# A graph attention kernel: head 0's second weight sum on VectorE, a quarter of the destinations made in another place, clamp and rounding constant on ScalarE

## The chip, the cores and the metric

The kernel runs on one core of a Trainium2 chip. The metric is the device time of one launch in microseconds. Three runs of the kernel before took 617.31, 618.71 and 619.45 us; the median is 618.71. The profile comes from one further execution.

## The reference, cut to what matters

Two graph attention layers over 512 nodes and 16,896 edges (8,192 in both directions and a loop on each node), then a residual and a layer norm. The first layer has 8 heads of 768 features, the second has one.

```python
def gat_layer(x, W, a_s, a_d, b, edge_index, concat):
    h = (x @ W).reshape(n, H, C)
    src, dst = (edge_index[0], edge_index[1])
    alpha_s = jnp.einsum('nhc,hc->nh', h, a_s)
    alpha_d = jnp.einsum('nhc,hc->nh', h, a_d)
    e = jax.nn.leaky_relu(alpha_s[src] + alpha_d[dst], NEG_SLOPE)
    m = jax.ops.segment_max(e, dst, num_segments=n)
    e = jnp.exp(e - m[dst])
    denom = jax.ops.segment_sum(e, dst, num_segments=n)
    alpha = e / (denom[dst] + EPS)
    msg = h[src] * alpha[:, :, None]
    out = jax.ops.segment_sum(msg, dst, num_segments=n)
    ...
h = gat_layer(x, W1, a_src1, a_dst1, b1, edge_index, concat=True)
h = jax.nn.elu(h)
out = gat_layer(h, W2, a_src2, a_dst2, b2, edge_index, concat=True)
return _layernorm(x + out)
```

x is 512x768, W1 768x6144, W2 6144x768, all in float32.

## The kernel before, in words

**Dense form of the graph.** The kernel first counts the edges between every pair of nodes into a dense matrix `cnt` (4 tiles of 128 destinations, 512 sources) on TensorE, as products of one-hot matrices. From then on attention is dense: a score per pair, minus infinity where no edge is (`absent`), a softmax weighted by the counts, and a 512x512 matrix product per head.

**Heads.** For each head h three dense products follow one another: the projection x·W1 of the next head, the aggregation of this head (scores times features, then the ELU), and its part of the second layer's projection. All are done by Strassen-like schemes in halves (7 products P1 to P7 in place of 8) or thirds, so sums of blocks of both operands are made ahead of the matmuls: sums of x, of features and of scores on VectorE, sums of weight blocks on VectorE or by DMAs that add onto what stands in the tile (`accum_op=ALU.add`, issued from GpSimd's queue).

**The order around the change.** `tc.manual_schedule()` is on: each engine runs its instructions in the order in which the program writes them. Head 0's projection (`first_projection`, L644) and the edge counting are written out together, in the loop at L855 over five batches of edge chunks. For a batch, VectorE makes the destinations of a quarter of the chunks (`destinations`, L779: L776 and L781, into `od`) and the one-hot rows of sources (L796); ScalarE makes other one-hot rows for the next batch (L794); TensorE runs the products that are due (`wants`, L846: 3 of them by the end of batch 0, 8 by batch 1, and so on) and, after batches 2 and 4, the counting matmuls (L822). `ahead_of` (L843) holds what VectorE does before batch 1: `weight_sums` and the first sum of x (`s1`, L419), then come the fresh quarter of destinations, `s2` (L420) and `s4` (L422). Results of a product that VectorE has to add (L664) are kept in `waiting` and run at the start of the next batch; the one of batch 0 runs at its end.

**Head 0's weight sums.** The weights stand as `W1[0]`: the lower and the upper half of the rows (`lo`, `hi`), each with left and right columns (L, R). The sums are

- t1 (P5) = lo L + lo R, on VectorE (L580),
- t2 (P6) = t1 + hi R: hi R is loaded a second time into t2 (`sums_by_dma`, L262 to L266), and a DMA adds t1 (L268),
- P7 = lo R + hi R, by a DMA from the weights in HBM onto lo R (L582),
- t4 (P4) = t2 + hi L, by a DMA (L269).

After these, in GpSimd's queue, come head 1's sums (L113, L121, L268, L269 with `slot="w2"`). TensorE takes head 0's products in the order P1, P2, P5, P3, P6, P7, P4 (two groups of matmuls each, one per half of the nodes; the profile shows both as one row of twelve matmuls). P3 reads hi R and `s4`.

**Counts in digits.** The counting matmuls pack four digits to the base 64 in one float. `counted_in_digits` (L602) takes them apart: `higher` on ScalarE scales by a power of 64 and adds a large rounding constant (L614), takes the constant off again for the highest digit (L616); `lower` on VectorE takes it off the two middle digits (L621) and subtracts what belongs to the higher digit (L622); `mask` on ScalarE writes `absent`. One tile is done after batch 2, the other three after the last batch, interleaved with the first products of head 1 and the first scores of head 0 (L932 to L941).

**Between the count and the first aggregation.** The loop at L1222 runs head 1's products 4 to 13 and beside them head 0's softmax: `leak` (L719), `rank` (L724 and the exponential L730), `give` (L1214: the denominator on VectorE, scaling and parting into halves of words on ScalarE, L1015 and L1018, then a transposing DMA from SP, L1020), and `turn_in` (L1023, ScalarE puts the transposed scores together in `PT`). At n == 9 GpSimd clamps three quarters of `cnt` at zero from below (L1229). The first aggregation, `near_first` (L1115), starts with three products P1 (`begin`, each copied to `u` by ScalarE, L1132); after the first of them stands `turn_in(3)`; then the sums, P2 on top of each P1, and the rest. Its argument `fill` names work to be written at places (c, j) in it. The first reader of the clamped counts is `logarithm` (L736), in head 0's turn of the loop at L1292, for head 1.

Of the kernel before, what the change touches and what calls it, by code (L numbers as in the profile page):

```python
# [39 lines left out]
def gat_pass(  # L40
# [217 lines left out]
    def sums_by_dma(W_, m, slot):  # L258

        lo_, hi_, t1_ = W_  # L260
        t2, t4 = (w1_halves[j] if slot == "w1" else wpool.tile([P, HK, HALF], F32, name=f"{slot}t{j}") for j in (2, 4))
        loads = [(t2, R), (t4, L)]  # L262
        if slot == "w1":
            loads.insert(1, (hi_[:, :, R], R))
        for t_, cols in loads:
            nc.sync.dma_start(t_, block(m, 1, cols))  # L266

        additions = [lambda: nc.gpsimd.dma_start(t2, t1_, accum_op=ALU.add),  # L268
                     lambda: nc.gpsimd.dma_start(t4, t2, accum_op=ALU.add)]  # L269
        return dict(P1=lo_[:, :, L], P2=hi_[:, :, L], P3=hi_[:, :, R], P4=t4, P5=t1_, P6=t2,  # L270
                    P7=lo_[:, :, R]), additions

    B0, additions0 = sums_by_dma(W1[0], w1_0, "w1")
# [178 lines left out]
    def half(t, j, h=0):  # L452
        return lambda: half_logits(h, t)[j]()
# [123 lines left out]

    def weight_sums():

        nc.vector.tensor_tensor(W1[0][2], W1[0][0][:, :, L], W1[0][0][:, :, R], op=ALU.add)  # L580
        additions0[0]()
        nc.gpsimd.dma_start(W1[0][0][:, :, R], block(w1_0, 1, R), accum_op=ALU.add)  # L582
        additions0[1]()
        load_w1(1, "w2")()
        B_, additions1 = sums_by_dma(W1[1], w1[:, D:2 * D], "w2")
        for f in additions1:
            f()
        return B_
# [13 lines left out]
    def counted_in_digits(t, ps, steps):  # L602
# [9 lines left out]
        def higher():  # L612
            for j in range(NT - 1, 0, -1):
                nc.scalar.activation(c[:, j * P:(j + 1) * P], whole, AF.Copy, bias=ROUND, scale=scale / BASE ** j)  # L614
                if j == NT - 1:
                    nc.scalar.activation(c[:, j * P:], c[:, j * P:], AF.Copy, bias=-ROUND, accum_out=sums[:, NT + t:NT + t + 1])  # L616
            if not steps:
                nc.scalar.activation(c[:, :P], whole, AF.Copy, scale=scale)

        def lower():  # L620
            nc.vector.tensor_scalar(c[:, P:3 * P], c[:, P:3 * P], -ROUND, None, op0=ALU.add)  # L621
# [135 lines left out]
    if not general:  # L757
# [85 lines left out]
        ahead_of = {1: [lambda: B1.update(weight_sums()), s1]}  # L843
# [11 lines left out]
        for n, batch in enumerate(batches):  # L855
# [53 lines left out]
            if n == 0:  # L909
                waiting.pop()()  # L910
# [14 lines left out]
        def given_lift(t):  # L925
            q.append(lift(0, t))

        def order_of(*fs):
            for f, *args in fs:
                f(*args)  # L930

        second_tile, step_tile, last_tile = deferred  # L932
        order_of(second_tile[:1], (item, 16), (half(0, 1),), second_tile[1:2], step_tile[:1], (item, 17), (spread, 0),
                 (half(1, 1),), step_tile[1:2], (given_lift, 0), last_tile[:1], second_tile[2:], (half(2, 1),))
        leak(q[0])
        given_lift(1)
        rank(q[0], 0)
        order_of(last_tile[1:2], (half(3, 1),), step_tile[2:], (given_lift, 2))
        leak(q[1])
        rank(q[1], 1)  # L940
        order_of(last_tile[2:], (given_lift, 3))  # L941
    else:
# [12 lines left out]
        turn_b1()  # L955
        B1 = weight_sums()
# [265 lines left out]
    for n in range(4, 14):  # L1222
# [5 lines left out]
        if n == 9 and not general:  # L1228
            nc.gpsimd.tensor_scalar(cnt[:, :, :3 * P], cnt[:, :, :3 * P], 0.0, None, op0=ALU.max)  # L1229
# [62 lines left out]
    for h in range(H - 1):  # L1292
# [14 lines left out]
        if h == 0:  # L1307
            GA, gsums = left(gT, gS)
            finish = near_first(0, AA, BB, [*rsums, lsums[3]], {(0, 1): [half(2, 0, 1)], (1, 1): sources[:1], (2, 1): [*sources[1:], *row, targets[0]]},
# [356 lines left out]
```

## Time and profile before

| what | value |
|---|---|
| runs, median (lowest to highest) | 618.71 us (617.31 to 619.45) |
| profiled execution, its own time | 617.82 us |
| its span, first to last instruction | 615.9 us |
| granted TensorE clock | 0.999 |
| mean DMA rate over the span | 207 GB/s |

Engines have short names: PE is TensorE's matmuls and PEld its weight loads, DVE is VectorE, ACT is ScalarE, POOL is GpSimd, SP is SyncE. A name with a q is the engine's sequencer. Rows of a timeline show the start and the duration in microseconds, the engine, the line of the kernel, the operation, the tile written and those read (without buffer numbers), the shape, how many instructions were merged, and in brackets how long the engine stood idle before and what ended that. Rows of the chain show a start, a duration and what filled it. A waits row shows who waited for whom: microseconds in total, how many times, the longest. A group's row ends in busy time, the mean nanoseconds of one, and the idle time before.

### The profile page before, as it was taken

Reading aid. Unit: us, or ns where it says so; the run is one execution under the profiler, and the core shown is the slowest. Engines: PE = TensorE matmul, PEld = TensorE weight load, DVE = VectorE, ACT = ScalarE, POOL = GpSimd, SP = SyncE. Lnnn points to the kernel's source line nnn. Section 1 sums busy time; section 2 is a strip of 40 time slices with the busy share of each in tenths; the row PEclk is TensorE's granted clock in tenths of the full one; section 3 lists DMA queues with packets and bytes.
Section 4 is the critical chain, followed back from the end, with each engine's and each line's share of the span. In section 5 each row is a group of like instructions: output and inputs, shape, how many; then the busy total and the mean of one; then the engine's idle time right before and its main releaser. Section 6 shows DMA issues by size and latency. Waiting matters only on the chain.

```text
span 615.9 us, 8599 instructions
## 1 busy us (share of the span) xinstructions
PE 605.7 (98%) x2772; PEld 481.7 (78%) x2772; DVE 527.0 (86%) x1152; ACT 332.0 (54%) x623; POOL 150.4 (24%) x184
## 2 busy tenths in 40 slices
PE   9999999999999999999999999999999999999995
PEld 6565685557888888888888888888888888885553
DVE  6999989887999879977897879978898878978785
ACT  5557866812766164932757055741857056753360
POOL 3210301032431332403341332413342303110000
PEclk9999999999999999999999999999999999999999
DMA  8994968799999998999899999999889993690032
GB/s 296 315 245 79 228 160 277 150 304 312 230 176 233 252 247 221 143 314 245 182 182 219 256 257 220 135 315 210 207 204 213 288 287 69 153 270 6 17 78 80
DMA packets 107836, 127.42 MB, mean 207 GB/s; under 512 B 41558, under 2 KB 87946, under 8 KB 107018
## 3 DMA queue, kind: packets, MB, share of 16 engines
q1 hardware_dynamic: 75213, 90.83, 48.7%
q0 software_dynamic: 32208, 35.59, 37.6%
q8 instruction: 24, 0.39, 0.2%
q10 hardware_dynamic: 365, 0.40, 0.2%
q14 instruction: 26, 0.21, 0.1%
HBM read 97.81 MB, written 2.90 MB: 164 GB/s over the span
## 4 chain that ended last, share of the span: by engine, by line
PE 90%; DMA 4%; DVE 3%; ACT 2%; SPq 0%; issue 0%; DVEq 0%; POOLq 0%
PE mm L521 46%; PE mm L1086 18%; PE mm L439 14%; PE mm L1126 5%; PE mm L1611 3%; PE held L439 2%; DMA w1t<-w1t 2%; DMA w1t<-in_L_gnn_W_dram 1%; DMA zr<-pS 1%; DMA w1r<-in_L_gnn_W_dram 1%; DVE scr L448 1%; ACT PT L1023 1%; PE tr L822 0%; ACT pS L1018 0%; DVE q L719 0%
## 5 line engine op out<-in xcount | busy, mean ns | idle before, releaser
L527 ACT ACTIVATE hs<-mm 128x512 f32<-128x512 f32 x30 | 17.9, 596 | 81.2 <-PE mm L521 80.8
L1086 PE MATMUL mm<-PT,hs 128*128 128x256 f32 x216 | 52.5, 379 | 0.0
L728 ACT ACTIVATE q<-q,nmax 128x512 f32<-128x512 f32 x32 | 23.1, 721 | 49.1 <-DVE nmax L724 48.9
L534 DVE TENSOR_TENSOR hs<-hs,mm 128x512 f32<-128x512 f32 x45 | 30.9, 686 | 18.6 <-PE mm L521 17.8
L1086 PEld LDWEIGHTS mm<-PT,hs 128*128 128x128 f32 x216 | 41.0, 190 | 5.8
L532 POOL DMA_DIRECT2D h<-pass x22 | 26.7, 1312 | 76.3 <-ACT pass L531 75.6
L1023 ACT COPY PT<-zr 128x1024 uint16<-128x1024 uint16 x34 | 39.4, 1158 | 8.8 <-DMA zr<-pS 5.8
L534 DVE TENSOR_TENSOR h<-h,mm 128x512 f32<-128x512 f32 x56 | 38.3, 684 | 5.8 <-PE mm L521 5.6
L521 PE MATMUL mm<-w2r,xT 128*128 128x256 f32 x160 | 37.8, 379 | 0.0
L521 PE MATMUL mm<-w2r,gT 128*128 128x256 f32 x160 | 37.0, 379 | 0.0
L1086 PE MATMUL mm<-pS,gS 128*128 128x256 f32 x144 | 37.0, 379 | 0.0
L136 POOL DMA_DIRECT2D w1t<-in_L_gnn_W_dram x18 | 30.1, 1945 | 26.0 <-DVE pS L1059 26.0
L521 PE MATMUL mm<-w1t,hs 128*128 128x256 f32 x144 | 34.1, 380 | 0.0
L521 PE MATMUL mm<-w1r,hs 128*128 128x256 f32 x144 | 34.0, 379 | 0.0
L521 PE MATMUL mm<-w1r,gS 128*128 128x256 f32 x144 | 34.0, 379 | 0.0
L136 POOL DMA_DIRECT2D w1r<-in_L_gnn_W_dram x12 | 14.5, 1207 | 79.6 <-DMA w1r<-in_L_gnn_W_dram 75.9
L521 PEld LDWEIGHTS mm<-w2r,gT 128*128 128x128 f32 x160 | 30.4, 190 | 4.1
L521 PEld LDWEIGHTS mm<-w2r,xT 128*128 128x128 f32 x160 | 30.4, 190 | 4.1
L521 PEld LDWEIGHTS mm<-w1t,hs 128*128 128x128 f32 x144 | 27.3, 190 | 3.9 <-ACT absent L531 0.2
L1086 PEld LDWEIGHTS mm<-pS,gS 128*128 128x128 f32 x144 | 27.4, 190 | 3.7
L521 PEld LDWEIGHTS mm<-w1r,gS 128*128 128x128 f32 x144 | 27.3, 190 | 3.7
L521 PEld LDWEIGHTS mm<-w1r,hs 128*128 128x128 f32 x144 | 27.2, 190 | 3.8
(328 smaller groups left out, 1561.1 us busy)
## 6 DMA issues: line engine op xcount, KB each, us to landing
w2r<-in_L_gnn_W_dram SPq DMA_DIRECT2D x48, 384.0 KB
w1r<-in_L_gnn_W_dram SPq DMA_DIRECT2D x43, 384.0 KB
w1t<-in_L_gnn_W_dram SPq DMA_DIRECT2D x24, 256.0 KB
h<-pass POOLq DMA_DIRECT2D x22, 256.0 KB, 6.9
gT<-xd SPq DMA_DIRECT2D x5, 1024.0 KB
w1t<-in_L_gnn_W_dram POOLq DMA_DIRECT2D x18, 256.0 KB, 7.2
a_s<-in_L_gnn_a_src_dram SPq DMA_DIRECT2D x8, 384.0 KB
a_d<-in_L_gnn_a_dst_dram SPq DMA_DIRECT2D x8, 384.0 KB
```

The lines of the kernel that those rows point to most:

```text
L136: nc.gpsimd.dma_start(o, i, accum_op=ALU.add)
L439: nc.tensor.matmul(ps[:, :HALF], A_[p][:, k, i * P:(i + 1) * P], B_[p][:, k, :], start=start and k == 0, stop=k == HK - 1, skip_group_chec ...
L448: return [lambda al=al, a=a, sign=sign: nc.vector.scalar_tensor_tensor(scr, HS[h][:, t, :], sign, a, op0=ALU.mult, op1=ALU.mult, accum_out ...
L521: nc.tensor.matmul(bank[chain][:, i * TH:(i + 1) * TH], A_[p][:, k, i * P:(i + 1) * P], B_[p][:, k, :], start=first and i == k == 0, stop= ...
L527: nc.scalar.activation(out(o), ps, AF.Copy, scale=sign)
L532: nc.gpsimd.dma_start(out(o), part, accum_op=ALU.add)
L534: nc.vector.tensor_tensor(out(o), out(o), ps, op=ALU.add if sign > 0 else ALU.subtract)
L728: nc.scalar.activation(q, q, AF.Exp, bias=nmax, scale=-1.0, accum_out=dens[t])
L1023: nc.scalar.copy(PT.rearrange("p s n -> p (s n)").bitcast(U16).rearrange("p (s n h) -> p s n h", s=NT, h=2)[:, :, t * P:(t + 1) * P, :], p ...
L1086: nc.tensor.matmul(bank[p][:, :HN], A_[p][:, k, c * P:(c + 1) * P], B_[p][:, k, :], start=over is None and k == 0, stop=k == 1, skip_group ...
L1126: nc.tensor.matmul(banks[c, p][:, :HN], A_[p][:, k, c * P:(c + 1) * P], B_[p][:, k, :], start=over is None and k == 0, stop=k == 1, skip_g ...
L1611: nc.tensor.matmul(ps[:, :cols.stop - cols.start], PT[:, s, t * P:(t + 1) * P], h2[:, s, cols], start=(s == 2), stop=(s == 1))
```

## The change

Four edits:

1. For head 0, hi R is no longer loaded into t2. VectorE adds t1 and hi R into t2, in `weight_sums`. The first sum (t1) becomes a function of its own, `first_sum`; VectorE's order before batch 1 is now t1, `s1`, t2, and then `s2` and `s4`. GpSimd's queue loses the DMA that added t1.
2. The quarter of destinations that batch 1 needs is made at the end of batch 0, before the waiting addition of L664.
3. The rounding constant of the two middle digits is taken off by ScalarE (at the end of the loop in `higher`), not by VectorE.
4. The clamp of `cnt` is a Relu on ScalarE, written in `near_first` at place (0, 0), not a GpSimd instruction at n == 9. The calls after the last count stand in another order.

```diff
-    def sums_by_dma(W_, m, slot):
+    def sums_by_dma(W_, m, slot, by_vector=False):
...
         loads = [(t2, R), (t4, L)]
-        if slot == "w1":
+        if by_vector:
+            loads[0] = (hi_[:, :, R], R)
+        elif slot == "w1":
             loads.insert(1, (hi_[:, :, R], R))
...
-        additions = [lambda: nc.gpsimd.dma_start(t2, t1_, accum_op=ALU.add),
-                     lambda: nc.gpsimd.dma_start(t4, t2, accum_op=ALU.add)]
+        def sum_t2():
+            if by_vector:
+                nc.vector.tensor_tensor(t2, t1_, hi_[:, :, R], op=ALU.add)
+            else:
+                nc.gpsimd.dma_start(t2, t1_, accum_op=ALU.add)
+        additions = [sum_t2, lambda: nc.gpsimd.dma_start(t4, t2, accum_op=ALU.add)]
...
-    B0, additions0 = sums_by_dma(W1[0], w1_0, "w1")
+    B0, additions0 = sums_by_dma(W1[0], w1_0, "w1", by_vector=True)
...
+    def first_sum():
+        nc.vector.tensor_tensor(W1[0][2], W1[0][0][:, :, L], W1[0][0][:, :, R], op=ALU.add)
+
     def weight_sums():
 
-        nc.vector.tensor_tensor(W1[0][2], W1[0][0][:, :, L], W1[0][0][:, :, R], op=ALU.add)
         additions0[0]()
...
+            nc.scalar.activation(c[:, P:3 * P], c[:, P:3 * P], AF.Copy, bias=-ROUND)
             if not steps:
                 nc.scalar.activation(c[:, :P], whole, AF.Copy, scale=scale)
 
         def lower():
-            nc.vector.tensor_scalar(c[:, P:3 * P], c[:, P:3 * P], -ROUND, None, op0=ALU.add)
...
-        ahead_of = {1: [lambda: B1.update(weight_sums()), s1]}
+        ahead_of = {1: [first_sum, s1, lambda: B1.update(weight_sums())]}
...
             if n == 0:
+                ((k,),) = [sorted({c // quarter for c in batches[1]} - made)]
+                made.add(k)
+                destinations(k)
                 waiting.pop()()
...
-        order_of(second_tile[:1], (item, 16), (half(0, 1),), second_tile[1:2], step_tile[:1], (item, 17), (spread, 0),
-                 (half(1, 1),), step_tile[1:2], (given_lift, 0), last_tile[:1], second_tile[2:], (half(2, 1),))
-        leak(q[0])
-        given_lift(1)
-        rank(q[0], 0)
-        order_of(last_tile[1:2], (half(3, 1),), step_tile[2:], (given_lift, 2))
-        leak(q[1])
-        rank(q[1], 1)
-        order_of(last_tile[2:], (given_lift, 3))
+        order_of(second_tile[:1], (item, 16), (half(0, 1),), second_tile[1:2], step_tile[:1], (item, 17), (spread, 0), (half(1, 1),),
+                 (given_lift, 0), step_tile[1:2], last_tile[:1], second_tile[2:], (half(2, 1),), (given_lift, 1), (leak_at, 0),
+                 (rank_at, 0), last_tile[1:2], step_tile[2:], (half(3, 1),), (given_lift, 2), (leak_at, 1), (rank_at, 1),
+                 last_tile[2:], (given_lift, 3))
...
-        if n == 9 and not general:
-            nc.gpsimd.tensor_scalar(cnt[:, :, :3 * P], cnt[:, :, :3 * P], 0.0, None, op0=ALU.max)
...
+            def floor():
+                if not general:
+                    nc.scalar.activation(cnt[:, :, :3 * P], cnt[:, :, :3 * P], AF.Relu)
+
-            finish = near_first(0, AA, BB, [*rsums, lsums[3]], {(0, 1): [half(2, 0, 1)], (1, 1): sources[:1], (2, 1): [*sources[1:], *row, targets[0]]},
+            finish = near_first(0, AA, BB, [*rsums, lsums[3]], {(0, 0): [floor], (0, 1): [half(2, 0, 1)], (1, 1): sources[:1], (2, 1): [*sources[1:], *row, targets[0]]},
                                 [lambda: turn_in(3)])
```

`leak_at` and `rank_at` call `leak` and `rank` for a tile that exists by then.

More of the change, by code (lines that the diff above doesn't have):

```diff
@@ L926, in given_lift, with leak_at, rank_at @@
             q.append(lift(0, t))
+        def leak_at(t):
+            leak(q[t])
+        def rank_at(t):
+            rank(q[t], t)
         def order_of(*fs):
@@ L955, in gat_pass @@
         turn_b1()
+        first_sum()
         B1 = weight_sums()
```

## The prediction, made before the changed kernel was run

> **What bounds the kernel now.** I read the page first, then the waits of TensorE, then the chain that ended last, and only then the timelines of single engines around the two places that the waits name.
>
> ```profile
> span 615.9 us, 8599 instructions
> ...
> PE 605.7 (98%) x2772; PEld 481.7 (78%) x2772; DVE 527.0 (86%) x1152; ACT 332.0 (54%) x623; POOL 150.4 (24%) x184
> ...
> PE 90%; DMA 4%; DVE 3%; ACT 2%; SPq 0%; issue 0%; DVEq 0%; POOLq 0%
> ```
>
> TensorE (PE) is busy for 98% of the span and carries 90% of the chain. Nothing in the change takes work from TensorE, so it can pay only where TensorE stands still. The other engines are named in 10% of the chain; the waits say where.
>
> ```profile
> PE held L439 <- DMA w1t<-w1t: 1.5, 1, 1.5
> ...
> PE mm L1126 <- ACT u L1132: 0.6, 2, 0.4
> ```
>
> Besides one ahead of the very first matmul, these are all the waits of TensorE that the profile lists. The first is for the second weight sum of head 0 (tile `w1t2`, operand P6). The second is in head 0's aggregation, for a ScalarE copy. TensorE's timeline gives their true size, since a matmul's listed end is modelled and starts are not:
>
> ```profile
> 16.55 4.03 PE L439 MATMUL mm<-w1t,xS 128*128 128x384 f32 x12
> 20.42 4.03 PE L439 MATMUL mm<-w1r,xS 128*128 128x384 f32 x12
> 25.98 4.14 PE L439 MATMUL held<-w1t,xS 128*128 128x384 f32 x12 [1.53 <-DMA w1t<-w1t]
> 30.05 0.26 PE L745 MATMUL mm<-ident,b_rows 48*128 48x48 f32 x1
> ...
> 50.36 4.14 PE L439 MATMUL mm<-w2t,xS 128*128 128x384 f32 x12
> ...
> 70.14 2.75 PE L1126 MATMUL mm<-PT,hs 128*128 128x256 f32 x12
> 73.32 1.13 PE L1126 MATMUL mm<-PT,hs 128*128 128x256 f32 x4 [0.43 <-ACT u L1132]
> 74.65 1.99 PE L1126 MATMUL mm<-PT,hs 128*128 128x256 f32 x8 [0.20 <-ACT u L1132]
> 76.48 1.03 PE L1126 MATMUL mm<-pS,gS 128*128 128x256 f32 x4
> ```
>
> Twelve matmuls of 384 columns take 20.42 - 16.55 = 3.87 us from start to start. The group at 20.42 is followed only at 25.98, so 5.56 - 3.87 = **1.69 us** are lost. For the second place the chain gives the rate, 15.14 us for 68 matmuls of 256 columns, 0.223 each:
>
> ```profile
> 16.00 9.93 DMA w1t<-w1t
> ...
> 48.83 0.22 DVE cnt L621
> ...
> 50.59 0.34 DVE cnt L621
> ...
> 53.74 0.21 DVE cnt L621
> ...
> 66.87 4.95 DMA zr<-pS
> ...
> 71.84 1.17 ACT PT L1023
> 73.00 0.27 ACT u L1132
> ...
> 74.33 0.28 ACT u L1132
> ...
> 74.65 15.14 PE mm L1126 x68
> ```
>
> 12, 4 and 8 matmuls should take 2.67, 0.89 and 1.78 us. They took 3.18 (70.14 to 73.32), 1.33 and 1.83, so 0.51 + 0.44 + 0.05 = **1.00 us** is lost. The same rows say why. TensorE waits for the ScalarE copies of `u`; these stand behind `turn_in` (L1023) in ScalarE's order; that one waits for a transposing DMA of 4.95 us; and the DMA comes at the end of a chain that runs through VectorE from the last count on, with L621 three times on it. The whole stake is therefore about 2.7 us.
>
> **Part 1: the second sum by VectorE.** Removed are a 576 KB load into `w1t2` and the accumulating DMA of 9.93 us that ends at 25.9. Added is one VectorE addition over 128x1152 elements. The first sum (L580) has the same shape:
>
> ```profile
> 13.29 0.56 DVE L664 TENSOR_TENSOR hs<-hs,mm 128x384 f32<-128x384 f32 x1 [1.96 <-PE mm L439]
> 13.83 1.36 DVE L580 TENSOR_TENSOR w1t<-w1r 128x1152 f32<-128x1152 f32 x1
> ...
> 16.25 0.72 DVE L776 TENSOR_TENSOR here<-rel,offsets 128x1088 bf16<-128x1088 f16 x1
> 17.00 1.29 DVE L781 TENSOR_TENSOR odw<-here,weight 128x2176 bf16<-128x2176 bf16 x1
> ...
> 19.20 0.96 DVE L422 TENSOR_TENSOR xS<-xT,xS 128x768 f32<-128x768 f32 x1
> ```
>
> It costs 1.36 us and stands behind the first x sum, at 16.25, where the quarter of destinations stood. It waits for the upper right block of the weights. TensorE read that block at 20.42 without a wait, when its load was still issued behind the removed one, so it has landed by then; now it comes one load earlier. The sum is ready near 17.6, seven microseconds before TensorE wants it at 24.3. Queued behind the add on VectorE are the x sums, of which L422 ended at 20.16 for the group at 20.42.
>
> That is where the moved quarter pays. L776 and L781 take 18.21 - 16.25 = 1.96 us (the next instruction, L420, starts at 18.21). They go ahead of L664 at 13.29, where VectorE idled for 1.96 us. So VectorE gains 1.96, pays 1.36, and the x sums come 0.6 us sooner instead of later. If the gap is a little too short, L664 and the first sum move by some 0.1 us, and the add's 0.6 covers it. Without that cover the x sums would come 1.36 late and the group at 20.42 about 1.1 late. TensorE's 1.69 goes entirely in the sum. Late next on TensorE's side are operand P7 (L582) and, in head 1, operand P6:
>
> ```profile
> L582 POOL DMA_DIRECT2D w1r<-in_L_gnn_W_dram x1: 1614/1614/1614, 16.8 to 16.8; - x1
> ...
> DMA to landing us min/median/max: 14.7/14.7/14.7
> ```
>
> ```profile
> 45.14 0.88 POOL L268 DMA_DIRECT2D w2t<-w2t  x1 [11.01 <-DMA w2t<-in_L_gnn_W_dram]
> 50.23 0.85 POOL L269 DMA_DIRECT2D w2t<-w2t  x1 [4.21 <-DMA w2t<-w2t]
> 66.04 4.08 POOL L1229 TENSOR_SCALAR cnt<-cnt 128x1536 f32<-128x1536 f32 x1 [14.96 <-DVE q L995]
> ```
>
> L582 landed at 16.8 + 14.7 = 31.5, in time for the group at about 32 but too late for one 1.7 us sooner. Now it is first in GpSimd's queue, behind the first sum alone (ended 15.2): with the same 14.7 us it lands at 29.9, before about 30.3. In head 1 the sum that L269 waited for was there at 50.23 and TensorE began at 50.36. A TensorE 1.7 us earlier wants it at 48.7. Its L268 waited for loads until 45.14, and these loads now have 576 KB and a transfer of 9.93 us less ahead of them; I take it that they come at least 1.7 us sooner, so nothing is lost. If they don't, the first gain is given back there (rival A).
>
> Is 1.36 us right for the add while GpSimd makes L582's descriptors? L776 and L781 ran at 16.25 and 17.00 beside L268 and L582 (16.0 to 18.4) in 0.72 and 1.29 us, no longer than their groups' means. The Trainium skill (SBUF — State Buffer, "Who interferes with whom") says that a VectorE operation with two SBUF inputs is blocked by a GpSimd instruction that reads SBUF, but infers that descriptor making only needs the write side. By a block the add would cost up to 1.36 + 1.61 = 2.97 us, the x sums would end 1.0 us later than at 20.16, and the first gain would shrink to 0.9 us, the sum to 1.9; by the row it is 1.36, which I take.
>
> **Part 2: rounding constant and clamp to ScalarE.** VectorE loses four L621, three of them after the last count and on the chain. From their starts there to the L622 behind them (49.14, 50.95, 54.05) pass 0.31 + 0.36 + 0.31 = 0.98 us; this is the gain. At least 3 x 0.21 = 0.63 goes. ScalarE gains four copies over 128x256 and one Relu over 128x1536:
>
> ```profile
> 45.00:57.00 12.00, 11.87 (x77) 7.27 (x70) 11.48 (x33) 8.26 (x27) 1.73 (x2) 1.00 0.54 108
> 57.00:70.00 13.00, 13.00 (x43) 7.51 (x42) 12.65 (x33) 11.99 (x15) 3.96 (x1) 1.00 0.57 109
> ```
>
> ```profile
> L1034 ACT ACTIVATE nl<-nl 128x256 f32<-128x256 f32 x48 | 19.5, 407 | 0.0
> ...
> L736 ACT ACTIVATE cnt<-cnt,tiny 128x1536 f32<-128x1536 f32 x1 | 1.6, 1562 | 0.0
> ```
>
> ```profile
> 80.59 0.72 ACT L1032 ACTIVATE nr<-zr,nb1T 128x512 f32<-128x512 f32 x1 [3.63 <-DVE zr L1168]
> ```
>
> (The columns of the stages are TensorE, its weight loads, VectorE, ScalarE and GpSimd.) Three copies are 3 x 0.41 = 1.2 us between 45 and 57, where ScalarE is idle for 12 - 8.26 = 3.7 us, so they cost nothing; without that room they would cost 1.2 us. The fourth is at the first count, where ScalarE waits for VectorE anyway. The Relu, 1.56 us, falls into the 3.63 us that end at 80.59. After 57 ScalarE is nearly full (11.99 of 13), so it can only move forward as a block, which it does when its inputs come 0.98 us earlier. The second wait needs just that: for the copies of `u` to be in time, the one at 74.33 must end 0.95 us earlier (74.65 against 72.81 + 0.89 = 73.70). So 0.98 covers **1.0 us**, barely; at 0.63 there would be 0.3 left of the wait.
>
> The Trainium skill (ScalarE: Activation LUTs, "Rules for kernel authors") speaks against this edit: relu and add belong on VectorE, which is faster per element. By that rule the chain would have 1.23 us of ScalarE where it has 0.22 + 0.34 + 0.21 = 0.77 us of VectorE, and the sum would be 0.5 us less than the first gain alone, 1.2. The rows go against the rule here, since ScalarE idles for 3.7 us.
>
> ```profile
> L1048 DVE TENSOR_TENSOR gS<-hs x8: 950/951/2910, 67.2 to 535.3; 128x768 f32<-128x768 f32 x8
> ```
>
> GpSimd's clamp, 4.08 us from 66.04, goes. Beside it, at 67.2, one VectorE subtraction took 2.91 us, and 0.95 in the median of its eight. These 1.96 us come back to VectorE between 67 and 70. TensorE isn't waiting for them: the chain there is a DMA. I count nothing for it; it gives VectorE room for the sums that follow. If the clamp were still needed sooner than the Relu now comes, the first reader, the logarithm for head 1, would wait; it stands behind the whole of this aggregation in ScalarE's own order, so it can't. The reordered calls at the end of the count leave the order on each engine as it was, so they count nothing either.
>
> **Sum.** 1.69 + 1.00 = 2.7 us off the profiled execution's 617.82 (span 615.9), which was 0.9 under the median of the runs shown. Against the median: 618.71 - 2.7 = **616.0 us**. After 76 us TensorE runs without a listed wait to the end, and loads are released by its progress, so what is gained stays.
>
> **Rivals.** *A: head 1's second sum is late.* The wait moves from 24 us to 50 us. For it: 50.23 against 50.36. Against: the DMA work removed ahead of it. Only the second gain stays: 618.71 - 1.0 = 617.7.
>
> *B: ScalarE takes VectorE's place.* The copies push ScalarE's work back, and the wait before 74.65 stays. For it: 11.99 of 13.00 us busy and an allowance of 0.03 us. Against: 3.7 idle us ahead. The rule of the Trainium skill quoted above points this way too. Only the first gain stays: 618.71 - 1.7 = 617.0.
>
> *C: slower; VectorE waits in order for the block.* If the load that the add waits for lands late, everything behind the add stands. The latest landing that the row at 20.42 allows makes the add wait 4.1 us (from 16.3).
>
> ```profile
> 16.00:45.00 29.00, 27.89 (x109) 1.00 1.08 287
> ```
>
> VectorE has 29.00 - 27.89 = 1.1 us idle until the last count, 0.6 us from the moved quarter and 0.3 from an L621, so the count would come 4.1 - 2.0 = 2.1 us late; the second gain gives 1.0 back: 618.71 + 1.1 = 619.8. It is slower than before from a landing at 16.3 + 2.0 + 1.0 = 19.3 on. Against it: the removed load was ahead of this one, and its own time is gone.
>
> **Chances.** Forecast 0.58, B 0.14, A 0.12, C 0.09, something unseen and slower 0.07. About 0.3%, 1.9 us, is what a measurement of this kernel can tell from no change, so the limit lies at 616.85. With the runs spread by about 1 us either way, the forecast gives 0.50 faster and 0.08 same; B 0.06 and 0.08; A 0.01 and 0.11; C 0.05 same and 0.04 slower; the unseen 0.07 slower. That makes 0.57 faster, 0.32 same and 0.11 slower. The range takes in the forecast, A and B with the runs' spread: from 614.8 (2.7 and 1.2 more) to 618.4.
>
> **What would show it.** TensorE's list of waits would lose both rows, the group behind the one at 20.42 would start near 24.3, and everything up to the last count would come 1.7 us sooner. VectorE would run L776 and L781 before its first L664 and the add near 16.3. ScalarE's `u` copies would end before TensorE's second operands want them. L1048 would take 0.95 us in every case. The prediction is wrong if a wait for `w2t` stands before head 1's third group, if the copy of `u` is still named, or if VectorE idles for a load before the add.

## The result and the profile after

The changed kernel takes 615.44 us in the median of 16 runs (614.74 to 617.33). The kernel before, run beside it 16 times, takes 617.75 (616.93 to 622.07). The ratio is 0.996 (95% interval 0.9947 to 0.9973), some 2.3 to 2.5 us less: faster by 0.4%, and by 0.27% at the interval's near end. The profiled execution took 615.07 us with a span of 613.0, against 617.82 and 615.9: 2.75 us less, or 2.9 by the spans.

The page of the kernel after has these lines for the three that opened the argument (span, busy time of each engine, shares of the chain that ended last):

```profile
span 613.0 us, 8592 instructions
...
PE 604.9 (99%) x2772; PEld 481.9 (79%) x2772; DVE 525.3 (86%) x1149; ACT 335.4 (55%) x628; POOL 145.5 (24%) x182
...
PE 97%; DVE 2%; ACT 1%; issue 0%; DVEq 0%
```

TensorE has the same 2772 matmuls and the same busy time within 0.8 us. The DMA's 4% has gone from the chain, and TensorE carries 97% of it. TensorE's waits are down to the one ahead of its first matmul:

```profile
PE bc L292 <- DVE zeros L286: 1.1, 1, 1.1
```

The lines of the changed kernel lie 6 to 13 lower than those of before: L439 is now L445, L664 is L672, L776 and L781 are L784 and L789, L1023 is L1036, L1126 is L1139. TensorE's timeline after, at the two places:

```profile
16.62 4.03 PE L445 MATMUL mm<-w1t,xS 128*128 128x384 f32 x12
20.50 4.03 PE L445 MATMUL mm<-w1r,xS 128*128 128x384 f32 x12
24.36 4.03 PE L445 MATMUL held<-w1t,xS 128*128 128x384 f32 x12
...
48.64 4.14 PE L445 MATMUL mm<-w2t,xS 128*128 128x384 f32 x12
...
68.42 5.34 PE L1139 MATMUL mm<-PT,hs 128*128 128x256 f32 x24
73.59 1.03 PE L1139 MATMUL mm<-pS,gS 128*128 128x256 f32 x4
```

From 20.50 the next group follows after 3.86 us, where it took 5.56: **1.70 us** came from the first place. From 68.42 to 73.59, the first product that reads a sum of scores, pass 5.17 us, where 70.14 to 76.48 took 6.34: **1.17 us** came from the second. Together they are 2.87 us, and the span is 2.9 shorter; the group at 20.50 itself started 0.08 later than in the profile of before.

VectorE's timeline after shows the new order. The quarter (L784, L789) stands ahead of the waiting addition L672, which starts at 13.37, and the new addition is L272:

```profile
11.27 0.72 DVE L784 TENSOR_TENSOR here<-rel,offsets 128x1088 bf16<-128x1088 f16 x1
12.02 1.29 DVE L789 TENSOR_TENSOR odw<-here,weight 128x2176 bf16<-128x2176 bf16 x1
...
16.33 1.35 DVE L272 TENSOR_TENSOR w1t<-w1t,w1r 128x1152 f32<-128x1152 f32 x1
...
18.58 0.96 DVE L428 TENSOR_TENSOR xS<-xT,xS 128x768 f32<-128x768 f32 x1
```

And ScalarE's timeline after shows the second place: `turn_in` (L1036), the copies of `u` (L1145) and the new Relu (L1322).

```profile
67.93 1.16 ACT L1036 COPY PT<-zr 128x1024 uint16<-128x1024 uint16 x1 [1.28 <-DMA zr<-pS]
69.48 0.37 ACT L1145 COPY u<-mm 128x256 f32<-128x256 f32 x1 [0.38 <-PE mm L1139]
...
74.12 1.50 ACT L1322 ACTIVATE cnt<-cnt 128x1536 f32<-128x1536 f32 x1
77.71 0.72 ACT L1045 ACTIVATE nr<-zr,nb1T 128x512 f32<-128x512 f32 x1 [2.08 <-DVE zr L1181]
```

### The profile page after: what moved, and what is told of

It is laid out like the page before. It is cut to its first block, busy times and chain, and to the rows that moved or that the text cites. A ratio compares the mean times of both kernels' runs of the same rounds, so it can differ in the third digit from the quotient of the medians.

```text
span 613.0 us, 8592 instructions
## 1 busy us (share of the span) xinstructions
PE 604.9 (99%) x2772; PEld 481.9 (79%) x2772; DVE 525.3 (86%) x1149; ACT 335.4 (55%) x628; POOL 145.5 (24%) x182
## 4 chain that ended last, share of the span: by engine, by line
PE 97%; DVE 2%; ACT 1%; issue 0%; DVEq 0%
PE mm L527 47%; PE mm L445 19%; PE mm L1099 18%; PE mm L1139 6%; PE mm L1626 3%; PE held L445 2%; PE bc L292 1%; DVE os L804 0%; PE tr L830 0%; DVE odw L789 0%; PE tr L1535 0%; DVE here L784 0%; ACT hs L484 0%; PE tr L1020 0%; PE mm L327 0%
## 5 line engine op out<-in xcount | busy, mean ns | idle before, releaser
L1036 ACT COPY PT<-zr 128x1024 uint16<-128x1024 uint16 x34 | 39.4, 1158 | 4.8 <-DMA zr<-nr 3.2
L527 PE MATMUL mm<-w2r,xT 128*128 128x256 f32 x160 | 37.8, 379 | 0.0
L527 PE MATMUL mm<-w2r,gT 128*128 128x256 f32 x160 | 37.0, 379 | 0.0
L527 PE MATMUL mm<-w1t,hs 128*128 128x256 f32 x144 | 34.1, 380 | 0.0
L527 PE MATMUL mm<-w1r,hs 128*128 128x256 f32 x144 | 34.0, 379 | 0.0
L527 PE MATMUL mm<-w1r,gS 128*128 128x256 f32 x144 | 34.0, 379 | 0.0
L527 PEld LDWEIGHTS mm<-w2r,xT 128*128 128x128 f32 x160 | 30.4, 190 | 4.1
L527 PEld LDWEIGHTS mm<-w2r,gT 128*128 128x128 f32 x160 | 30.4, 190 | 4.1
L527 PEld LDWEIGHTS mm<-w1t,hs 128*128 128x128 f32 x144 | 27.3, 190 | 3.9 <-ACT absent L537 0.2
L527 PEld LDWEIGHTS mm<-w1r,gS 128*128 128x128 f32 x144 | 27.3, 190 | 3.7
L527 PEld LDWEIGHTS mm<-w1r,hs 128*128 128x128 f32 x144 | 27.2, 190 | 3.8
```

What stands on the lines that cost most here:

```text
L527: nc.tensor.matmul(bank[chain][:, i * TH:(i + 1) * TH], A_[p][:, k, i * P:(i + 1) * P], B_[p][:, k, :], start=first and i == k == 0, stop= ...
L1036: nc.scalar.copy(PT.rearrange("p s n -> p (s n)").bitcast(U16).rearrange("p (s n h) -> p s n h", s=NT, h=2)[:, :, t * P:(t + 1) * P, :], p ...
```

## The experiments

The theory was that of the prediction: the first sum's wait is worth 1.7 us, the shorter chain after the count some 1.0, and the clamp nothing. The rivals were that the second wait goes with the first, that ScalarE or a load takes the place of the wait that went, and that the second wait's end is a matter of the transposing DMA and not of VectorE's chain.

Three lengths are read from every profile at the second place. One is TensorE's time from the first P1 of the aggregation to the first product with a sum of scores; without a wait it is about 5.17 us. The second, **D**, runs from the start of SP's third transposing DMA to the start of the `turn_in` copy that waits for it. In the kernel after it is 67.93 - 63.91 = 4.02 us. The third, the **lead**, runs from the start of that DMA to TensorE's first P1, and says how early the DMA is sent; in the kernel after it is 68.42 - 63.91 = 4.51 us. SP's timeline after has the DMA and the two loads ahead of it:

```profile
61.78 0.52 SPq L226 DMA_DIRECT2D a_s<-in_L_gnn_a_src_dram  x1
62.39 0.39 SPq L226 DMA_DIRECT2D a_d<-in_L_gnn_a_dst_dram  x1
63.91 1.24 SPq L1033 DMA_TRANSPOSE zr<-pS  x1
```

### The second sum alone

The kernel after, with the rounding constant back on VectorE and the clamp back on GpSimd at n == 9.

```diff
-            nc.scalar.activation(c[:, P:3 * P], c[:, P:3 * P], AF.Copy, bias=-ROUND)
...
         def lower():
+            nc.vector.tensor_scalar(c[:, P:3 * P], c[:, P:3 * P], -ROUND, None, op0=ALU.add)
...
+        if n == 9 and not general:
+            nc.gpsimd.tensor_scalar(cnt[:, :, :3 * P], cnt[:, :, :3 * P], 0.0, None, op0=ALU.max)
...
-            finish = near_first(0, AA, BB, [*rsums, lsums[3]], {(0, 0): [floor], (0, 1): [half(2, 0, 1)],
+            finish = near_first(0, AA, BB, [*rsums, lsums[3]], {(0, 1): [half(2, 0, 1)],
```

> The changed kernel with its rounding constant back on VectorE and its clamp back on GpSimd: the second sum by VectorE and the moved quarter alone. Theory of two separate waits: TensorE loses the first wait (1.7 us) and keeps the second (1.0 to 1.2 us, with the copy of u named), so 1.7 us under the kernel before, a ratio of 0.9973 and a span near 614.2. Rival, the second wait hung on the first (fewer DMAs, or VectorE's 0.6 us, free it too): 2.8 us under, span near 613.1, no wait at the copy of u.

615.54 us in the median of 5 runs, ratio 0.9962 (0.9949 to 0.9975); the kernel before took 618.26 in the runs beside it, here and in the three timed kernels that follow. The first wait is gone. In TensorE's timeline a wait for `u` is left, and the chain has the transposing DMA back:

```profile
68.34 3.93 PE L1139 MATMUL mm<-PT,hs 128*128 128x256 f32 x16
72.48 1.99 PE L1139 MATMUL mm<-PT,hs 128*128 128x256 f32 x8 [0.21 <-ACT u L1145]
74.31 1.03 PE L1139 MATMUL mm<-pS,gS 128*128 128x256 f32 x4
```

```profile
64.94 4.69 DMA zr<-pS
```

It takes 5.97 us to the first sum product: 0.80 are lost, though VectorE's chain is as long as before, when 1.17 were. So the first part pays without the second, and in these runs nearly all that both pay; the second wait has another cause beside VectorE's chain.

### ScalarE's part alone

The kernel before, with the rounding constant and the clamp on ScalarE and nothing else.

```diff
+            nc.scalar.activation(c[:, P:3 * P], c[:, P:3 * P], AF.Copy, bias=-ROUND)
...
-            nc.vector.tensor_scalar(c[:, P:3 * P], c[:, P:3 * P], -ROUND, None, op0=ALU.add)
...
-            nc.gpsimd.tensor_scalar(cnt[:, :, :3 * P], cnt[:, :, :3 * P], 0.0, None, op0=ALU.max)
...
+            def floor():
+                if not general:
+                    nc.scalar.activation(cnt[:, :, :3 * P], cnt[:, :, :3 * P], AF.Relu)
...
```

> The kernel before with only the rounding constant and the clamp on ScalarE. Theory of two separate waits: the wait for the second weight sum stays (1.5 us listed), the one for the copy of u goes; 1.0 to 1.2 us under the kernel before, a ratio near 0.998, span near 614.8. Rival, ScalarE takes VectorE's place: the copy of u is still named and the time is that of before, span 615.9.

617.09 us, ratio 0.999 (0.9979 to 1.0001): 0.6 us less by the ratio, 1.2 between the medians, and no change lies within the interval. TensorE's list keeps the first wait, with 1.6 us, and loses the one for `u`; its timeline at the second place shows 5.33 us.

```profile
70.14 5.50 PE L1126 MATMUL mm<-PT,hs 128*128 128x256 f32 x24
75.47 1.03 PE L1126 MATMUL mm<-pS,gS 128*128 128x256 f32 x4
```

The profile shows the second gain as forecast, with a D of 5.21 us, longer than the 4.97 of the kernel before. By the ratio the runs show little more than half of it. This kernel doesn't have the calls after the last count in their new order, and its lead is 4.52 us, as in the kernel after: the new order adds nothing to it.

### The quarter of destinations left in its place

```diff
             if n == 0:
-                ((k,),) = [sorted({c // quarter for c in batches[1]} - made)]
-                made.add(k)
-                destinations(k)
                 waiting.pop()()
```

> The changed kernel with the quarter of destinations back between the weight sums and the second x sum. Theory, VectorE binds from there to the last count: TensorE's group after 20.5 starts about 1.0 us late, VectorE's 1.96 us less its 0.3 idle make the last count 1.6 us late, and the span is near 614.6. Rival, only TensorE's own wait counts and VectorE catches up: 1.0 us over the changed kernel, span near 614.0. Second rival, it is hidden: 613.0.

616.73 us, ratio 0.9982 (0.9968 to 0.9996). Its profiled execution lay 1.5 us above that median, because the first weights came late there: in VectorE's timeline the first sum itself (L585) waits 2.12 us for the load of `w1r`. So the same kernel was profiled once more.

> The same kernel as e3_no_move once more, for a profile: there the first weight sum stood 2.1 us for the load of a weight block, which comes ahead of what that kernel changes. Theory, that wait was of the execution: without it the group after 16.6 starts on time, the one after 20.5 about 1.0 us late, the last count about 1.6 us late and the span is near 614.6. Rival, the wait comes with the quarter's old place: it is there again and the span is near 616.3.

615.8 us, span 613.8, and no such wait: it belongs to the execution and not to the place of the quarter. What stays is seen in VectorE's and TensorE's timelines of this second profile:

```profile
20.12 0.96 DVE L428 TENSOR_TENSOR xS<-xT,xS 128x768 f32<-128x768 f32 x1
```

```profile
16.20 4.03 PE L445 MATMUL mm<-w1t,xS 128*128 128x384 f32 x12
21.18 4.11 PE L445 MATMUL mm<-w1r,xS 128*128 128x384 f32 x12 [0.94 <-ACT hs L670]
```

The releaser that the row names is not the one. The last sum of x ends at 21.08, and the group that reads it starts at 21.18, 4.98 us after the one before instead of 3.87: 1.11 us are lost. The prediction had named "about 1.1" for this group without the move. The last count, expected 1.6 us late, came 0.97 later on the clock (46.80 in place of 45.83) and 1.39 later if counted from the group at 16.20. Timed, the move is worth 0.9982 against 0.996, some 1.4 us between runs of different series, with intervals that overlap.

### The clamp left on GpSimd

```diff
+        if n == 9 and not general:
+            nc.gpsimd.tensor_scalar(cnt[:, :, :3 * P], cnt[:, :, :3 * P], 0.0, None, op0=ALU.max)
...
-            finish = near_first(0, AA, BB, [*rsums, lsums[3]], {(0, 0): [floor], (0, 1): [half(2, 0, 1)],
+            finish = near_first(0, AA, BB, [*rsums, lsums[3]], {(0, 1): [half(2, 0, 1)],
```

> The changed kernel with the clamp on GpSimd again, the rounding constant on ScalarE. Theory, the clamp only delays a VectorE subtraction that TensorE isn't waiting for: L1061's first instruction takes 1.3 to 2 us longer (2.2 to 2.9 us), TensorE waits nowhere, span 613.0 as in the changed kernel. Rival, VectorE's lost time reaches TensorE through the score sums: up to 2 us over, span near 615.

615.18 us, ratio 0.9961 (0.9948 to 0.9973): the same as the kernel after. VectorE's subtraction beside the clamp is again stretched, and TensorE does not feel it (5.18 us from 68.41 to 73.59):

```profile
64.89 2.21 DVE L1061 TENSOR_TENSOR gS<-hs 128x768 f32<-128x768 f32 x1
```

The clamp's move costs and brings nothing that shows.

### The rounding constant left on VectorE

```diff
-            nc.scalar.activation(c[:, P:3 * P], c[:, P:3 * P], AF.Copy, bias=-ROUND)
...
         def lower():
+            nc.vector.tensor_scalar(c[:, P:3 * P], c[:, P:3 * P], -ROUND, None, op0=ALU.add)
```

> The changed kernel with the rounding constant back on VectorE and the clamp left on ScalarE. Theory, the three subtractions on the chain after the last count are the whole second gain: the same loss as with both undone, TensorE's first group of the aggregation's sums 5.97 us after its first P1 (5.17 in the changed kernel), span near 613.7. Rival, GpSimd's clamp was part of the second wait: 5.2 us and a span near 613.1.

615.19 us, ratio 0.9961 (0.9945 to 0.9978), with 617.68 for the kernel before in these runs and in those of the next two. With VectorE's chain as long as before, TensorE loses 0.18 us at the second place, not 1.0:

```profile
68.26 5.51 PE L1139 MATMUL mm<-PT,hs 128*128 128x256 f32 x24
73.61 1.03 PE L1139 MATMUL mm<-pS,gS 128*128 128x256 f32 x4
```

D was 4.09 us here, 0.9 less than in the kernel before. So the wait for `u` all but goes when the DMA happens to be short, as it does when the chain is shortened. The rival, that GpSimd's clamp has a part in the wait by way of D, is neither shown nor ruled out: D lies between 4.72 and 4.99 us in the four profiles with the clamp on GpSimd and the loads in their old place, and between 3.94 and 5.21 in the eight with the clamp on ScalarE. (This profiled execution has a wait of 1.2 us at 403 us, `mm` of L527 for ScalarE, that the profile of after does not have; it took 616.68.)

### The load of the upper right block given back

The kernel after with the 576 KB load back ahead of the block that VectorE's addition waits for. The loaded data isn't used: the addition overwrites it.

```diff
         if by_vector:
-            loads[0] = (hi_[:, :, R], R)
+            loads.insert(1, (hi_[:, :, R], R))
```

> The changed kernel with the removed 576 KB load put back ahead of the block that the new addition reads; VectorE then overwrites what it loaded. Theory, the accumulating transfer was the wait and the load only takes room that is there: the block lands by about 17, the addition slips by less than 0.9 us, which the x sums have to spare, and head 1's second sum is there before TensorE wants it near 48.6; span 613.0. Rival C, VectorE stands in order for the block and pushes the group after 20.5 and the last count back: 1 to 2 us over. Rival A, head 1's sum is late at 48.6: a wait for w2t there, up to 1.7 us over.

616.04 us, ratio 0.9972 (0.9962 to 0.9982). VectorE now waits for loads, 0.68 us ahead of the first sum (L585) and 1.00 ahead of the new addition, and TensorE's next group starts late. The first of these is not the edit's alone: the kernel after had one of 0.59 us in its second profile, without the load.

```profile
17.68 1.36 DVE L272 TENSOR_TENSOR w1t<-w1t,w1r 128x1152 f32<-128x1152 f32 x1 [1.00 <-DMA w1r<-in_L_gnn_W_dram]
```

```profile
21.01 4.11 PE L445 MATMUL mm<-w1r,xS 128*128 128x384 f32 x12
```

This is rival C's mechanism in small: the group starts 0.5 us later than in the kernel after. The median is 0.6 higher, but from another series, and the intervals of the ratios overlap. Without that load the block is there when VectorE comes to the addition at 16.33.

### The new copy on ScalarE made twice

```diff
             nc.scalar.activation(c[:, P:3 * P], c[:, P:3 * P], AF.Copy, bias=-ROUND)
+            nc.scalar.activation(c[:, P:3 * P], c[:, P:3 * P], AF.Copy, bias=0.0)
```

> The changed kernel with a second ScalarE copy (adding zero) behind each new one, so the price that ScalarE pays is doubled: four more copies of 0.42 us (0.3 in a row). Theory, ScalarE has the room: three of them add 0.9 to 1.3 us where it idled 3.7 us before the change and some 2.4 after it, the copies of u move by at most 0.5 us and TensorE waits nowhere or up to 0.2 us; span 613.0 to 613.3. Rival B, ScalarE is the bound there: every added copy comes out at the copies of u, 0.9 to 1.3 us over, span 613.9 to 614.3.

615.58 us, ratio 0.9974 (0.9955 to 0.9992). The copies of `u` come in time (5.18 us). TensorE waits at a place that no theory had named, for ScalarE's copy of head 1's second product:

```profile
48.88 4.14 PE L445 MATMUL mm<-w2t,xS 128*128 128x384 f32 x12 [0.50 <-ACT hs L484]
```

In the kernel after that copy runs from 48.10 to 48.58, directly behind a new L625 copy, and the group starts at 48.64. So the change used up ScalarE's room at exactly this place: one more copy of 0.42 us is a listed wait of 0.50. By the starts 0.37 us are lost, 1.11 from the transposes at 47.77 to this group where 0.74 are usual.

### The loads of the attention vectors moved away from the transposing DMA

In SP's queue the third transposing DMA stands behind two loads of 384 KB (L226, in the rows of D above). They were put ahead of the first transposing DMA, in the kernel before and in the kernel after, and both kernels were run again beside these. The kernel before took 618.57 us in these runs.

```diff
+    load_a(1, a_src1[1], a_dst1[1])
     for n in range(4, 14):
...
-        if n == 6:
-            load_a(1, a_src1[1], a_dst1[1])
```

> The kernel before with one edit: the two attention-vector loads of head 1 (768 KB together) are issued ahead of head 0's first transposing DMA, where they stood between the second and the third. VectorE's chain, its four subtractions and GpSimd's clamp stay. Theory, the second wait is as long as the third transposing DMA stands behind these loads in SP's queue: the DMA takes about 2.7 us in place of 4 to 5, as the first one does, the copies of u are in time and TensorE's wait there goes; 1.0 to 1.2 us under the kernel before, a span near 614.8. Rival, VectorE's chain alone sets it: the wait at the copy of u stays at 0.6 us as listed, span 615.9.

In the kernel before the edit changes nothing that can be measured: 618.38 us, ratio 0.9989 (0.9973 to 1.0005). The 1.0 to 1.2 us that were expected don't show, and the interval, which reaches 1.7 us less, doesn't rule them out. In the profile the second wait goes as the theory says (72.09 to 77.27, 5.18 us), without any of the change. D is 3.12 us, where all the kernels with the loads in their old place have 3.9 to 5.2, and the lead is 3.40, much as the 3.27 in the first profile of the kernel before. GpSimd's clamp ran beside this short DMA as well (67.86 to 71.94), so it doesn't lengthen the DMA by itself:

```profile
68.69 1.23 SPq L1020 DMA_TRANSPOSE zr<-pS  x1
...
71.81 1.17 ACT L1023 COPY PT<-zr 128x1024 uint16<-128x1024 uint16 x1 [0.39 <-DMA zr<-pS]
...
72.09 5.34 PE L1126 MATMUL mm<-PT,hs 128*128 128x256 f32 x24
77.27 1.04 PE L1126 MATMUL mm<-pS,gS 128*128 128x256 f32 x4
```

But its profiled execution took 620.28 us. Most of this is lost at the first place (another 0.9 us is a wait of TensorE for ScalarE at 408.71): the wait for the sum is 1.91 us long there, and the group behind it takes 5.76 us (to 31.98) instead of 4.07. The clock is what differs; in the windows the column behind the five engines is the granted TensorE clock:

```profile
26.22 5.83 PE L439 MATMUL held<-w1t,xS 128*128 128x384 f32 x12 [1.91 <-DMA w1t<-w1t]
```

```profile
26.00:28.00 2.00, 1.78 (x4) 1.04 (x5) 2.00 (x14) 1.46 (x5) 1.54 (x2) 0.69 1.10 287
28.00:30.00 2.00, 2.00 (x5) 1.08 (x4) 1.33 (x5) 0.00 (x0) 0.67 (x1) 0.50 1.11 303
```

> The changed kernel with the same edit. Theory, nothing is left to win in an execution whose transposing DMA is short, since TensorE waits nowhere there: span 613.0, and a median within 0.3 us of the changed kernel's in this call, at best a little lower by the executions in which the DMA is long. Rival, the changed kernel's other executions do wait at the copy of u: 0.3 to 0.6 us lower.

In the kernel after the edit brings 615.39 us, ratio 0.995 (0.9931 to 0.9969), with a D of 3.12 us again, and 5.18 us at the second place, as without it. The median is 0.28 us under that of the kernel after beside it, which the spread of their runs doesn't tell from nothing.

> The changed kernel once more, beside its variant on the same chip: span near 613.0, a ratio of 0.996 within its interval, and the third transposing DMA between 3.9 and 5.2 us. If it is near 5 here, a wait at the copy of u of at most 0.2 us.

The kernel after again: 615.67 us, ratio 0.9937 (0.9918 to 0.9956). D is 4.55 us this time, half a microsecond more than in its first profile, and no wait for `u` comes of it (5.18 us).

> The kernel before once more, for a second profile. If the transposing DMA's length is of the execution, TensorE's loss between the first P1 of the aggregation and the first product with a sum (6.34 us in the first profile) is 5.17 us plus what the DMA takes above about 3.9: near 5.3 us at 4.0 and 6.3 at 5.0. If it is of the kernel, it is 6.3 again.

The kernel before again, one execution: 616.94 us, span 615.0, 0.9 us less than its first profile. TensorE's timeline tells why this execution differs:

```profile
24.81 4.14 PE L439 MATMUL held<-w1t,xS 128*128 128x384 f32 x12 [0.47 <-DMA w1t<-w1t]
...
48.74 0.60 PE L698 MATMUL tr<-ident,wide 128*128 128x128 f32 x4
50.13 4.11 PE L439 MATMUL mm<-w2t,xS 128*128 128x384 f32 x12 [0.79 <-ACT q L715]
...
69.88 3.62 PE L1126 MATMUL mm<-PT,hs 128*128 128x256 f32 x16
73.66 1.99 PE L1126 MATMUL mm<-PT,hs 128*128 128x256 f32 x8 [0.16 <-ACT u L1132]
75.49 1.03 PE L1126 MATMUL mm<-pS,gS 128*128 128x256 f32 x4
```

Head 0's sum came early, a wait of 0.47 in place of 1.53. TensorE then reached head 1's second sum before it was there: the group at 50.13 stands 1.39 us behind the transposes, where 0.74 are usual (49.62 to 50.36 in the first profile), so 0.65 are lost. The ScalarE instruction that the row names is not what it waited for: in the first profile it ran until 50.95, and the same group started at 50.36. GpSimd's next sum, which waits for the same DMA, starts at 50.28.

```profile
50.28 0.85 POOL L269 DMA_DIRECT2D w2t<-w2t  x1 [4.21 <-DMA w2t<-w2t]
```

This is rival A's mechanism, in the kernel before itself. At the second place 5.61 us pass with a D of 4.99, where 6.3 had been expected: the expectation took the wait to follow from D alone, but the delay in head 1 had moved TensorE back against the chain, and the lead was 4.03 us in place of 3.27.

## Why the prediction was right, point by point

**First wait, 1.69 us: right.** The start to start shows 1.70. The sum without the rest of the change brings 0.38% (0.25 to 0.51), 2.7 us between the medians, more than its 1.70 and the 0.37 that its profile saves at the second place. The kernel before has a spread of its own here: its first wait was 1.53, 0.47 and, with the loads moved, 1.91 us, once with a half clock behind it and once with a wait in head 1. The profile of before on which the sum was built is one of these, neither the best nor the worst. The mean granted clock that is on record with each run gives a hint of the half clock's share: it is 0.993 to 0.995 in 9 of 98 runs of the kernels with this sum by DMA and in 1 of 91 with the sum by VectorE, and all ten took more than 619 us. Where in those runs the clock fell is not known but for the one profile, so the shares of the median stay open.

**The new addition, 1.36 us at 16.25, unblocked: right.** It took 1.35 at 16.33. GpSimd made L590's descriptors from 15.66 to 17.14 beside it, so the block by GpSimd that the prediction set against the row did not occur here.

```profile
15.66 1.48 POOL L590 DMA_DIRECT2D w1r<-in_L_gnn_W_dram  x1 [8.50 <-DVE w1t L585]
...
39.16 0.91 POOL L274 DMA_DIRECT2D w2t<-w2t  x1 [11.58 <-DMA w2t<-in_L_gnn_W_dram]
45.17 0.86 POOL L275 DMA_DIRECT2D w2t<-w2t  x1 [5.11 <-DMA w2t<-w2t]
```

**The moved quarter pays for it: right.** It ran from 11.27 to 13.31, filled the gap, and the last sum of x ended at 19.54, not at 20.16. Without the move 1.1 us are lost at one group.

**What is late next: right, with more room than assumed.** P7's load landed 12.8 us after its issue at 15.66, at 28.5, before 30.26. Head 1's loads let L274 start at 39.16 instead of 45.14, 6 us sooner where 1.7 was taken; the sum was there at 45.17 and wanted at 48.64. Rival A was refuted for the kernel after, and seen in the kernel before.

**L621's worth, 0.98 us: too small.** From the first correction of the count to head 1's additions VectorE takes 7.95 us (45.83 to 53.78 in the last two rows below), where the same stretch took 9.21 before (47.54 to 56.75). That is 1.26. The prediction took L621's starts from the chain (48.83, 50.59, 53.74). By VectorE's timeline they lie at 48.75, 50.51 and 53.65, and to the L622 behind them pass 0.39 + 0.44 + 0.40 = 1.23 us.

```profile
47.54 0.28 DVE L607 TENSOR_TENSOR cnt<-cnt,bc 128x127 f32<-128x127 f32 x1
...
48.75 0.29 DVE L621 TENSOR_SCALAR cnt<-cnt 128x256 f32<-128x256 f32 x1
...
50.51 0.41 DVE L621 TENSOR_SCALAR cnt<-cnt 128x256 f32<-128x256 f32 x1
...
53.65 0.29 DVE L621 TENSOR_SCALAR cnt<-cnt 128x256 f32<-128x256 f32 x1
...
56.75 0.55 DVE L479 TENSOR_TENSOR hs<-hs,mm 128x384 f32<-128x384 f32 x1
```

```profile
45.83 0.28 DVE L615 TENSOR_TENSOR cnt<-cnt,bc 128x127 f32<-128x127 f32 x1
...
53.78 0.55 DVE L485 TENSOR_TENSOR hs<-hs,mm 128x384 f32<-128x384 f32 x1
```

**Second wait, 1.00 us: too small as well.** The rate from the chain, 0.223 us for a matmul, put the 24 matmuls up to the first sum product at 5.34 us. Undisturbed they take 5.17, 0.215 each, so 6.34 - 5.17 = 1.17 us were lost in the profile of before.

**"So 0.98 covers 1.0 us, barely": true for that profile, and by luck.** Both sizes were some 0.2 us short, and the errors cancelled: 1.17 had to be covered, and the lead grew by 4.51 - 3.27 = 1.24. What was wrong is the reason. The step took the transposing DMA's 4.95 us as fixed, and so the wait as a property of the chain. D differs from one execution to the next. In the six profiles in which TensorE is held up, the first sum product starts 4.64 or 4.65 us after the `turn_in` copy, so it can't come sooner than 4.64 + D - lead after the first P1, nor sooner than TensorE's own 5.17:

| kernel | rounding constant by | lead, us | D, us | 4.64 + D - lead | to the first sum product, us |
|---|---|---|---|---|---|
| before, first profile | VectorE | 3.27 | 4.97 | 6.34 | 6.34 |
| before, second | VectorE | 4.03 | 4.99 | 5.60 | 5.61 |
| second sum alone | VectorE | 3.40 | 4.72 | 5.96 | 5.97 |
| rounding left on VectorE | VectorE | 3.38 | 4.09 | 5.35 | 5.35 |
| before, loads moved | VectorE | 3.40 | 3.12 | 4.36 | 5.18 |
| ScalarE's part alone | ScalarE | 4.52 | 5.21 | 5.33 | 5.33 |
| quarter not moved, first profile | ScalarE | 4.32 | 4.92 | 5.24 | 5.25 |
| clamp on GpSimd | ScalarE | 4.51 | 4.79 | 4.92 | 5.18 |
| copy made twice | ScalarE | 4.38 | 4.58 | 4.84 | 5.18 |
| after, second profile | ScalarE | 4.53 | 4.55 | 4.66 | 5.18 |
| load given back | ScalarE | 4.35 | 4.43 | 4.72 | 5.18 |
| after, first profile | ScalarE | 4.51 | 4.02 | 4.15 | 5.17 |
| quarter not moved, second | ScalarE | 4.34 | 3.94 | 4.24 | 5.18 |
| after, loads moved | ScalarE | 4.55 | 3.12 | 3.21 | 5.18 |

In all fourteen profiles the last column is the larger of the two, to 0.01 us. So TensorE waits only when D is more than 0.53 us longer than the lead. With the loads in their old place the constant on VectorE costs 0.18 to 1.17 us. With the constant on ScalarE the lead is 4.3 to 4.6 us, and the loss never exceeds 0.16 us, even at the longest D.

**The sum, 1.69 + 1.00 = 2.7 us: right in size, with luck in the runs.** The two profiles show 2.87. Timed, the first part alone brings 2.3 us by its ratio, and both bring 2.3 to 2.5. ScalarE's part alone brings 0.1%, with no change inside its interval, and the kernel with the constant left on VectorE can't be told from the kernel after. So the second term is shown in profiles, and in the runs it is not shown on top of the first. The interval of the first part (1.5 to 3.2 us less) holds its 1.69 too, so the split of the gain between the two stays open.

**Clamp, nothing: right for the kernel after.** The Relu took 1.50 us at 74.12, and 2.08 us of idle time were left behind it. **ScalarE's room: right for the places named** (rival B did not occur), but the tightest place was another, the copy at 48.10, which no step had priced.

**The time.** 616.0 was forecast against a median of 618.71. Over 16 runs the kernel before lies at 617.75, 0.96 lower, and the kernel after at 615.44, 0.56 under the forecast. The gain was 0.4 less than forecast and the start 0.96 lower, so that the time comes out so near is luck in part.

## What to carry to other kernels

Take a wait's price from the starts around it, and then ask whether the length behind it belongs to the program or to the execution: the new addition took 1.35 or 1.36 us in every profile here, the transposing DMA 3.9 to 5.2. For a wait behind such a DMA, measure two things in several profiles: how long the DMA takes and how early it is sent. A gain in front of it makes the second longer and is paid only where the first is longer still, so its price is a range and not the one profile's number. And when work goes to an engine "with room", look for the one copy on it that another engine waits for, not at the idle share of the stretch.

## What the runs showed of the hardware that had not been expected

- **A transposing DMA behind two loads.** The same 128x1024 transposition took 3.94 to 5.21 us from issue to use in twelve profiles (D above), and 3.12 in both profiles with the loads ahead of all the transpositions. So the loads lengthen it, by 0.8 to 2.1 us; by which means was not shown.
- **Half clock after a short stop.** After a listed wait of 1.91 us the granted clock was 0.50 from 28 to 30 us, and twelve matmuls took 1.7 us more. After waits of 1.53 and 1.64 us at the same place it was 1.00. That the wait brought the lower clock about is likely by the order in time, but not shown. The Trainium skill (TensorE: Matmul & The Clock Gate, "Part 1: The HAM clock gate") puts the return to the lower clock after at least one idle window of about 3.4 us. The stop measured here was shorter, so for this kernel the measurement decides, though it is from one execution.
- **A releaser that is not the one.** Two of the rows above name a ScalarE instruction (L670, L715) where TensorE waited for something else: once for the last sum of x, which ended 0.10 us before the group started, and once for the sum by DMA whose next reader on GpSimd started 0.15 us after the group. The start of the waiting instruction, set against the ends of its other inputs, tells the true one.
